# State-space layers on Trainium2: from tiles of 128 channels with one state per row to tiles of 32 channels by four states

## The chip, the cores and the metric

The kernel runs on one core of one Trainium2 chip. A core has five engines with instruction queues of their own: TensorE (PE, matrix products), VectorE (DVE), ScalarE (ACT, functions), GpSimd (POOL) and SyncE (SP, which here only issues DMA transfers). Each works through its queue strictly in order and waits on semaphores for the others. SBUF is the on-chip memory with 128 partitions (rows), PSUM the accumulator memory of TensorE, DRAM the memory outside. The metric is the device time of one execution in microseconds (us), and a kernel's time is the median of its runs.

## The reference

Eight images of 384 channels and 32 x 32 pixels go through four layers, each of the form x = x + f(norm(x)). Layers 0 and 2 are state-space (Mamba) layers; layer 2 has a two-matrix MLP behind it. Layer 1 is a deformable convolution and layer 3 a shift by rounded offsets with a small blur. Only layers 0 and 2 are changed. Cut to what matters, one of them is, for a sequence of 1024 tokens:

```python
u  = silu(causal_conv3(in_proj(x)))            # 768 channels
dt, B, C = x_proj(u)                           # 24, 16 and 16 values a token
dt = softplus(dt @ dt_proj_w.T + bias)         # 768 channels
h  = exp(dt[d] * A[d, n]) * h + (dt[d] * u[d]) * B[n]    # token by token, 16 states n
y[d] = sum over n of h[d, n] * C[n]
out = out_proj((y + D * u) * silu(z))
```

The line for h is a recurrence over the tokens for each of 768 x 16 pairs of channel d and state n. Everything is float32.

## The kernel before

The layers run one after the other. A state-space layer is worked in **half-samples**: 8 images by two halves of 512 tokens make 16 steps. In a step the 768 channels are 6 groups of 128, one channel a partition, and the 16 states are taken two at a time. So a step has 6 x 8 = 48 **units** (s, j, m): half-sample s, channel group j, state pair m. I call the eight units of one j a **block**; a layer has 96 blocks and 768 units. A tile of a unit is 128 partitions by 2 states by 512 tokens (128x1024).

One unit is this chain:

- `decays` (L434, ACT): two activations exp(dt * A), one for each state, into PSUM (tile `da`, two buffers).
- `inputs` (L440, POOL): dt*u (tile `du`) times the rows B of this pair (tile `bc`), into `db` (three buffers).
- `scan` (L445, DVE): the recurrence, one tensor_tensor_scan over 1024 elements.
- `with_c` (L461): the result times C, on DVE, or on POOL for the units m that the table `GP_C` names (0 and 4 in layer 0, 0 in layer 2).
- `add_pair` (L469, POOL, layer 2 only): for the units of `GP_ADD` (1, 2, 3, 5, 6) the two states are added into one half of the tile.
- `read_out` (L474, PE): the states are summed by products with the identity matrix that accumulate in the PSUM tile `y`; two products a unit, one where the pair was added. In layer 0 a product with diag(D) opens the sum.

In the second half of a sample, small operations (`first_token`, `carry`, `add_carry`) bring the last state of the first half in. All 16 rows of B and C of a step are broadcast to 128 partitions by eight DMAs of 1 MB (`load_bc`, L382), eight `bc` tiles in all.

The step sizes of a block are made by `dt_proj` (PE), `soft_exp` and `soft_ln` (ACT), `soft_rest` (DVE) and `soft_sum` (L408, three POOL operations; the second finishes `dt`, the third makes `du`). Both tiles stay in SBUF in the form in which the units use them.

The order on PE, DVE, ACT and POOL is the order of the program text. The unit loop runs the pipeline ahead by hand: in iteration i POOL does `inputs` of unit i + 3 and ACT `decays` of unit i + 2, while DVE does `scan` of unit i. All other work of the step (projections, convolution, norms, the MLP of the step before) is put into lists by `plan` (L592), indexed by the unit at which it is issued. For a block that begins at unit t, the step sizes for the block **two further on** are made at t + 6 to t + 10: `soft_sum` is in the POOL list at t + 10, behind that iteration's `inputs`. Their first users are `inputs` of unit t + 16, which POOL issues in iteration t + 13, and `decays` of the same unit, which ACT issues in iteration t + 14. SP issues the loads and stores.

Of the kernel before, what the change touches and what calls it, by code (L numbers as in the profile page):

```python
# [30 lines left out]
GP_C = {0: (((0, 4), (0, 4)), ((0, 4), (0, 4))), 2: (((0,), (0,)), ((0,), (0,)))}  # L31
GP_ADD = {0: (), 2: (1, 2, 3, 5, 6)}
# [3 lines left out]
KS = (3, 5, 7)  # L36
CPP = 8
# [39 lines left out]
Q_YN, Q_XN, Q_SRC, Q_ONE, Q_EPS, Q_K, Q_BIG = 0, 8, 9, 18, 19, 20, 23  # L77
# [14 lines left out]
class Net:  # L92
# [107 lines left out]
    def ssm_layer(self, li, src, dst, shift=None):  # L200
        tc, nc, ins = self.tc, self.nc, self.ins
        mlp = li == 2
        gp_c, gp_add = GP_C[li], GP_ADD[li]
        nhs = 4 if mlp else 6
        with ExitStack() as ctx:
# [36 lines left out]
            na = wp.tile([P, ND, NS], F32, name="na")  # L242

            def states():
                naf = na.rearrange("p d n -> p (d n)")
                nc.scalar.activation(naf, vec[:, V_A : V_A + ND * NS], AF.Exp)
                nc.vector.tensor_scalar(naf, naf, -1.0, -1e-20, ALU.mult, ALU.min)
# [5 lines left out]
            def w_in(o):  # L253
                if not mlp:
                    return win[:, :, o * P : (o + 1) * P]
                t = p2.tile([P, G, P], F32, name="winr", tag="winr", bufs=3)
                nc.sync.dma_start(out=t, in_=win_d[:, :, o * P : (o + 1) * P])
                return t

            def w_mid(src, k):  # L260
                t = p2.tile([P, k, W_MID // k], F32, name="wm", tag="wm", bufs=3)
                n = src.shape[2]
                nc.sync.dma_start(out=t[:, :, :n], in_=src)
                return t
# [61 lines left out]
            def inner(s, d):  # L326
# [4 lines left out]
                xn, w = s["xn"], w_in(d)  # L331
# [42 lines left out]
            def x_store(s):  # L374
                ps = s["ps_x"]
                dbc = s["dbc"] = p1.tile([RB, TS], F32, name="dbc")
                nc.scalar.copy(dbc, ps)
                bcd = s["bcd"] = self.dram.tile([2, NS, TS], F32, name="bcd", tag="bcd")
                nc.sync.dma_start(out=bcd.rearrange("t n l -> (t n) l"), in_=dbc[RK:RB, :])
                s["bc"] = {}  # L380

            def load_bc(s, m):  # L382
                bc = s["bc"][m] = p2.tile([P, 2, 2, TS], F32, name="bc", tag="bc", bufs=NS // 2)
                nc.sync.dma_start(out=bc, in_=s["bcd"][:, 2 * m : 2 * m + 2, :].partition_broadcast(P))
# [7 lines left out]
            def soft_exp(s, j):  # L392
                bias, ps = v(V_DB + j), s["ps_dt"]
                s["dt", j] = dt = p2.tile([P, TS], F32, name="dt", tag="dt")
# [13 lines left out]
            def soft_sum(s, j):  # L408
                dt = s["dt", j]
                s["du", j] = du = p2.tile([P, TS], F32, name="du", tag="du")  # L410
# [5 lines left out]

            def first_token(s, j):
                dt = s["dt", j]
                if s["h"] == 1:
                    s["a0"] = p1.tile([P, NS], F32, name="a0")  # L420
                    nc.scalar.activation(s["a0"], na[:, j, :], AF.Exp, scale=dt[:, 0:1])
                nc.scalar.activation(dt[:, 0:1], self.col(Q_BIG), AF.Identity)

            def carry(s, j):
                if s["h"] == 1:
                    nc.gpsimd.tensor_tensor(s["a0"], s["a0"], s["st"][:, j, :], ALU.mult)

            def add_carry(s, j, m):
                if s["h"] == 1:
                    d = s["db", m][:, :, 0:1]  # L430
                    nc.gpsimd.tensor_tensor(d, d, s["a0"][:, 2 * m : 2 * m + 2].unsqueeze(2), ALU.add)  # L431


            def decays(s, j, m):  # L434
                da = s["da", m] = dap.tile([P, 2, TS], F32, name="da", tag=f"da{m % 2}")
                for i in range(2):
                    n = 2 * m + i
                    nc.scalar.activation(da[:, i, :], s["dt", j], AF.Exp, scale=na[:, j, n : n + 1])  # L438

            def inputs(s, j, m):  # L440
                db = s["db", m] = p2.tile([P, 2, TS], F32, name="db", tag="db", bufs=3)
                du = s["du", j].unsqueeze(1).to_broadcast([P, 2, TS])
                nc.gpsimd.tensor_tensor(db, du, s["bc"][m][:, 0], ALU.mult)  # L443

            def scan(s, j, m):  # L445
# [3 lines left out]
                h = da  # L449
                if m in gp_c[s["h"]][j % 2]:  # L450
                    h = s["hs", m] = p2.tile([P, 2, TS], F32, name="hs", tag="hs", bufs=nhs)
# [4 lines left out]
            def keep_last(s, j, m):  # L456
                if s["h"] == 0:
                    h = s["h", m]
                    nc.scalar.copy(s["sib"]["st"][:, j, 2 * m : 2 * m + 2].unsqueeze(2), h[:, :, TS - 1 : TS])  # L459

            def with_c(s, j, m):  # L461
                c = s["bc"][m][:, 1]
                if m in gp_c[s["h"]][j % 2]:
                    nc.gpsimd.tensor_tensor(s["hs", m], s["hs", m], c, ALU.mult)  # L464
                else:
                    hs = s["hs", m] = p2.tile([P, 2, TS], F32, name="hs", tag="hs", bufs=nhs)
                    nc.vector.tensor_tensor(hs, s["da", m], c, ALU.mult)  # L467

            def add_pair(s, j, m):  # L469
                hs = s["hs", m]  # L470
                nc.gpsimd.tensor_tensor(hs[:, 0, :], hs[:, 0, :], hs[:, 1, :], ALU.add)  # L471


            def read_out(s, j, m):  # L474
                k = s["read"] = (s.get("read", -1) + 1) % NU
                first = k == 0
                if first:
                    s["y"] = yp.tile([P, TS], F32, name="y", tag="y")
                    if not mlp:
                        nc.tensor.matmul(s["y"], diag_d[:, j, :], s["u"][:, j, :], start=True, stop=False)  # L480
                        first = False
                n = 1 if m in gp_add else 2
                for i in range(n):
                    nc.tensor.matmul(  # L484
                        s["y"], self.ident, s["hs", m][:, i, :],
                        start=first and i == 0, stop=k == NU - 1 and i == n - 1,
                    )

            def z_proj(s, j):
                w = w_in(ND + j)  # L490
# [20 lines left out]
            def out_proj(s, o, k0, k1):  # L511
                if k0 == 0:
                    wo = w_mid(wout_d[:, :, o * P : (o + 1) * P], ND) if mlp else wout[:, :, o * P : (o + 1) * P]
                    s["out", o] = self.psum("ps_o"), wo
# [25 lines left out]
            def mlp_up(s, q, f):  # L540
                if f == 0:
                    s["w1"] = w_mid(w1_d[:, :, q * 4 * P : (q + 1) * 4 * P], G)
                s["up", f] = ps = self.psum("ps_h")
                for k in range(G):
                    nc.tensor.matmul(  # L545
                        ps, s["w1"][:, k, f * P : (f + 1) * P], s["t"][:, k, :], start=(k == 0), stop=(k == G - 1)
                    )

            def up_take(s, q, f):
                if f == 0:  # L550
                    if s is steps[-1] and q == 1:
                        t = p2.tile([P, 2, 2, TS], F32, name="hid1", tag="bc", bufs=NS // 2)
                        s["hid"] = t.rearrange("p a b l -> p (a b) l")
# [8 lines left out]
            def mlp_down(s, q, o):  # L562
                if o == 0:
                    s["w2"] = w_mid(w2_d[:, 4 * q : 4 * q + 4, :], 4)
                s["down", o] = ps = self.psum("ps_m")
                for f in range(4):
                    nc.tensor.matmul(  # L567
                        ps, s["w2"][:, f, o * P : (o + 1) * P], s["hid", q][:, f, :], start=(f == 0), stop=(f == 3)
                    )

            def down_take(s, q, o):
# [5 lines left out]
                if q == NF // 4 - 1:  # L577
                    store(s, o)

# [12 lines left out]
            def plan(prev, s, nxt):  # L592
# [6 lines left out]
                for j in range(ND):  # L599
                    t = NU * j  # L600
                    put(dve, t + 1, close, *((s, j - 1) if j else (prev, ND - 1)))
                    put(pe, (0, 9, 18, 27, 33, 41)[j], z_proj, s, j)
# [11 lines left out]
                    put(pool, t + 10, soft_sum, n, k)  # L614
                put(pe, 0, norm_load, nxt)
# [20 lines left out]
                for d, t in enumerate((15, 16, 17, 24, 25, 26)):  # L636
                    put(pe, t, inner, nxt, d)
# [5 lines left out]
                for m in range(NU):  # L643
                    put(pool, 41 + m, load_bc, nxt, m)
                put(act, 7 if mlp else 9, residual, prev)
                for o, (t, e) in enumerate(((1, 2), (3, 4), (5, 6)) if mlp else ((8, 9), (10, 11), (12, 13))):
                    put(pe, t, out_proj, prev, o, 0, ND // 2)
                    put(pe, e, out_proj, prev, o, ND // 2, ND)
                    put(act if mlp else dve, e + (1 if mlp else 2), out_take, prev, o)
                if mlp:  # L650
                    ups = ((7, 8, 11, 13), (22, 23, 28, 29), (37, 38, 39, 40))
                    downs = ((19, 20, 21), (34, 35, 36), (43, 44, 45))
                    for q, g in enumerate((17, 33, 42)):
                        for f, t in enumerate(ups[q]):
# [14 lines left out]
            with tc.manual_schedule(engines=ENGINES):  # L669
# [10 lines left out]
                for d in range(ND):  # L680
                    inner(s, d)
# [10 lines left out]
                for j in range(2):  # L692
                    for fn in (dt_proj, soft_exp, soft_rest, soft_ln, soft_sum):
                        fn(s, j)
                for m in range(NU):
                    load_bc(s, m)
# [8 lines left out]
                for i, (s, j, m) in enumerate(units):  # L705
# [10 lines left out]
                    mine = m in gp_c[s["h"]][j % 2]  # L716
                    for r in early.pop(i, ()):
                        read_out(*units[r])
# [20 lines left out]
                    if m in gp_add:  # L739
                        add_pair(s, j, m)  # L740
                    run(pool[t])
                    run(pe[t])
                    for r in late.pop(i, ()):
                        read_out(*units[r])
                    k = 3 if mine else 2 if m in gp_add else 1
                    (early if k > 1 or m == NU - 1 else late).setdefault(i + k, []).append(i)
                for r in sum((early.get(len(units) + k, []) for k in range(3)), []):
                    read_out(*units[r])
                close(s, ND - 1)
                residual(s)  # L750
                if mlp:
                    parts = self.shift_parts(wp, p2, dap, dst, *shift)
# [3 lines left out]
                    for i in range(6):  # L756
                        stat_load(i)
                    stats = list(range(last))
                for o in range(G):
                    out_proj(s, o, 0, ND)  # L760
                    out_take(s, o)
                if mlp:
                    kernels_a()

                    def some(n):
                        for _ in range(min(n, len(stats))):
# [3 lines left out]
                            if i + 6 < last:  # L770
                                stat_load(i + 6)
# [3 lines left out]
                    for q in range(NQ + 1):  # L775
                        if q < NQ:
                            for f in range(4):
# [1070 lines left out]
```

## Time and profile before

| what | value |
|---|---|
| median of 3 runs (lowest to highest) | 9387.92 us (9382.41 to 9391.77) |
| profiled execution: span from first to last instruction | 9392.0 us; no longer time is recorded for it |
| layer 0, units (62 to 2974 us) | 2912 us, 30.33 us a block |
| layer 2, units (5915 to 9112 us) | 3197 us, 33.30 us a block |
| busy share of the span: PE, DVE, ACT, POOL | 90%, 86%, 69%, 62% |
| DMA moved | 791.97 MB, 84 GB/s over the span |

The span is 4 us (0.04%) above the median, so a difference worked out on the profiled execution can be put on the median as it stands. The POOL share over the span is low because POOL has little to do in layer 1 (about 3000 to 5830 us); in the unit stages of the two state-space layers PE, DVE and POOL are all busy for around nine tenths of the time. A float32 product shows as two matmul instructions in the trace. PE's busy time is modelled, since its products overlap at their ends.

### The profile page before, as it was taken

Reading aid. Unit: us, or ns where it says so; the run is one execution under the profiler, and the core shown is the slowest. Engines: PE = TensorE matmul, PEld = TensorE weight load, DVE = VectorE, ACT = ScalarE, POOL = GpSimd, SP = SyncE. Lnnn points to the kernel's source line nnn. Section 1 sums busy time; section 2 is a strip of 40 time slices with the busy share of each in tenths; the row PEclk is TensorE's granted clock in tenths of the full one; section 3 lists DMA queues with packets and bytes.
Section 4 is the critical chain, followed back from the end, with each engine's and each line's share of the span. In section 5 each row is a group of like instructions: output and inputs, shape, how many; then the busy total and the mean of one; then the engine's idle time right before and its main releaser. Section 6 shows DMA issues by size and latency. Waiting matters only on the chain. (4 is left out here: it accounts for less than half of the span.)

```text
span 9392.0 us, 87221 instructions
## 1 busy us (share of the span) xinstructions
PE 8473.1 (90%) x27891; PEld 4507.2 (48%) x27916; DVE 8088.9 (86%) x8857; ACT 6489.3 (69%) x10147; POOL 5825.4 (62%) x3825
## 2 busy tenths in 40 slices
PE   7898888888887999999999997699999999999987
PEld 3333333333333677677777776244343443434333
DVE  7999999999996678778778777899999999999973
ACT  6666666666663778778778777667777777777750
POOL 7989999999896000000000000899999999999974
PEclk9999999999998999999999998799999999999998
DMA  2111211121121233333333333233232333322436
GB/s 98 63 57 47 85 57 50 58 81 53 50 82 45 74 82 87 90 81 88 90 83 87 90 80 92 88 103 99 92 95 88 119 116 97 94 92 91 126 98 128
DMA packets 566063, 791.97 MB, mean 84 GB/s; under 512 B 244242, under 2 KB 397234, under 8 KB 542040
## 3 DMA queue, kind: packets, MB, share of 16 engines
q1 hardware_dynamic: 503492, 775.85, 28.2%
q10 hardware_dynamic: 62100, 10.44, 0.6%
q8 instruction: 223, 3.65, 0.2%
q14 instruction: 248, 2.03, 0.1%
HBM read 716.49 MB, written 69.66 MB: 84 GB/s over the span
## 5 line engine op out<-in xcount | busy, mean ns | idle before, releaser
L443 POOL TENSOR_TENSOR db<-du,bc 128x1024 f32<-128x1024 f32 x1536 | 3607.7, 2356 | 290.0 <-DVE hs L453 164.1
L453 DVE TENSOR_TENSOR_SCAN da<-da,db 128x1024 f32<-128x1024 f32 x1248 | 2857.4, 2290 | 125.1 <-ACT da L438 64.1
L484 PE MATMUL y<-hs,ident 128*128 128x512 f32 x5184 | 2598.4, 637 | 377.5 <-DVE hs L467 216.9
L438 ACT ACTIVATE da<-dt,na 128x512 f32<-128x512 f32 x3072 | 2120.8, 691 | 812.2 <-DVE hs L467 665.2
L411 POOL TENSOR_TENSOR dt<-dt,sp_e 128x512 f32<-128x512 f32 x192 | 244.3, 1272 | 2929.8 <-DVE sp_e L403 2929.8
L484 PEld LDWEIGHTS y<-hs,ident 128*128 128x128 f32 x5184 | 1013.1, 202 | 1853.0 <-issue 1094.2
L1516 PE MATMUL wacc<-fsm,fxk 128*128 128x221 f32 (+34 forms) x10624 | 1658.9, 315 | 96.5 <-DVE fsm L1486 93.8
L1516 PEld LDWEIGHTS wacc<-fsm,fxk 128*128 128x128 f32 x10624 | 1571.3, 195 | 234.9 <-DVE fsm L1486 157.6
L467 DVE TENSOR_TENSOR hs<-da,bc 128x1024 f32<-128x1024 f32 x1248 | 1528.5, 1225 | 91.6 <-DVE da L453 1.4
L1486 DVE TENSOR_TENSOR fsm<-fhy,fhx 128x170 f32<-128x170 f32 (+42 forms) x3216 | 1173.1, 436 | 342.9 <-PE wacc L1516 315.6
L1446 ACT ACTIVATE fhy<-fpyx,cell 128x416 f32<-128x416 f32 (+9 forms) x1280 | 646.8, 578 | 383.5 <-DVE fsm L1486 383.5
L1469 DVE TENSOR_TENSOR fxk<-fxt,fwk 128x1024 f32<-128x1024 f32 (+1 forms) x688 | 789.4, 1186 | 10.3 <-ACT fxt L1248 10.3
L453 DVE TENSOR_TENSOR_SCAN hs<-da,db 128x1024 f32<-128x1024 f32 x288 | 656.9, 2281 | 52.0 <-POOL db L431 35.8
L464 POOL TENSOR_TENSOR hs<-hs,bc 128x1024 f32<-128x1024 f32 x288 | 678.7, 2356 | 32.7 <-ACT st L459 32.3
L471 POOL TENSOR_TENSOR hs<-hs 128x512 f32<-128x512 f32 x480 | 610.0, 1271 | 4.6 <-DVE hs L467 4.1
L545 PE MATMUL ps_h<-t,wm 128*128 128x512 f32 x1152 | 538.5, 605 | 16.8 <-DVE x L574 16.6
L567 PE MATMUL ps_m<-hid,wm 128*128 128x512 f32 x1152 | 525.3, 600 | 20.1 <-ACT hid L560 17.2
L1451 ACT ACTIVATE fhy<-fhy,cols 128x1344 f32<-128x1344 f32 (+10 forms) x368 | 531.4, 1444 | 12.0
L459 ACT COPY st<-da 128x2 f32<-128x2 f32 x624 | 98.2, 157 | 512.0 <-DVE hs L467 509.8
L1157 PE MATMUL ps_off<-fxn,fow 128*98 128x465 f32 (+10 forms) x896 | 386.6, 579 | 0.0
L1433 ACT ACTIVATE fhx<-fpyx,cell 128x544 f32<-128x544 f32 (+8 forms) x640 | 380.7, 668 | 0.0
L567 PEld LDWEIGHTS ps_m<-hid,wm 128*128 128x128 f32 x1152 | 217.3, 192 | 314.8 <-issue 252.5
(203 smaller groups left out, 9866.3 us busy)
## 6 DMA issues: line engine op xcount, KB each, us to landing
bc<-bcd SPq DMA_DIRECT2D x256, 1024.0 KB
fpyx<-fposd SPq DMA_DIRECT2D x640, 256.0 KB
wm<-in_w SPq DMA_DIRECT2D x96, 768.0 KB
x<-x SPq DMA_DIRECT2D x71, 768.0 KB
winr<-in_win SPq DMA_DIRECT2D x192, 192.0 KB
x<-in_x SPq DMA_DIRECT2D x40, 768.0 KB
fpyx<-fposd SPq DMA_DIRECT2D x24, 1024.0 KB
wm<-in_wout SPq DMA_DIRECT2D x48, 384.0 KB
```

Source lines behind the costliest of these rows:

```text
L438: nc.scalar.activation(da[:, i, :], s["dt", j], AF.Exp, scale=na[:, j, n : n + 1])
L443: nc.gpsimd.tensor_tensor(db, du, s["bc"][m][:, 0], ALU.mult)
L453: nc.vector.tensor_tensor_scan(h1, da1, db1, 0.0, ALU.mult, ALU.add)
L464: nc.gpsimd.tensor_tensor(s["hs", m], s["hs", m], c, ALU.mult)
L467: nc.vector.tensor_tensor(hs, s["da", m], c, ALU.mult)
L471: nc.gpsimd.tensor_tensor(hs[:, 0, :], hs[:, 0, :], hs[:, 1, :], ALU.add)
L484: nc.tensor.matmul(s["y"], self.ident, s["hs", m][:, i, :], start=first and i == 0, stop=k == NU - 1 and i == n - 1,)
L567: nc.tensor.matmul(ps, s["w2"][:, f, o * P : (o + 1) * P], s["hid", q][:, f, :], start=(f == 0), stop=(f == 3))
L1446: nc.scalar.activation(hy[:, at : at + (yb - ya) * W], pyx[:, 0, ya * W : yb * W], AF.Abs, bias=bias)
L1469: nc.vector.tensor_tensor(t[:, :n], x, wk[:, j : j + 1, :].to_broadcast([P, n, P]), ALU.mult)
L1486: nc.vector.tensor_tensor(self.sub(sm, at, [(r * w, n), (w, r), (1, w)]), self.sub(hy, hy_at[by] + xa, [(r * W, n), (W, r), (1, w)]), self ...
L1516: nc.tensor.matmul(a[:, ya - 4 * o : yb - 4 * o, xa:xb], k, self.sub(sm, sm_at[by], [(w, yb - ya), (1, w)]), start=False, stop=False,)
```

## The change

The same 768 units a layer are cut differently. A tile now holds **four states by 32 channels** on the partitions and two further states along the free dimension; unit m = (p, k) covers channels 32k to 32k + 31 of the block's 128 and the eight states of half p. The elementwise operations of a unit keep their shapes (128x1024, two 128x512 activations).

- `dt` and `du` of a block are needed on every quarter of the partitions for four sub-blocks of 32 channels. `spread` stores both to DRAM (two stores of 256 KB) and loads each four times, to partitions 0 to 31, 32 to 63, 64 to 95 and 96 to 127 (eight loads of 256 KB in rows of 2 KB), into `dtb` and `dub`, two buffers each. It stands in the POOL list at t + 11, and SP issues its ten DMAs.
- `load_bc` brings only the four state rows that a quarter needs: two tiles a step, each by four loads of 256 KB. `bc` has three buffers instead of eight.
- `read_out` runs once for each half p, when its four units are done: eight products of a constant 128x32 selection matrix with the tiles. Product k writes partitions 32k to 32k + 31 of `y`, so four products use four column groups of PE. A block has 16 of them in both layers. `add_pair` is gone.
- `GP_C` is now 0 and 4 in layer 0, as before; in layer 2 it is 0, 2, 4 for even blocks and 0, 4 for odd ones.
- The loads of weight tiles (`fetch_in`, `fetch`) are issued two units ahead of the products that use them. `first_token` in a second half does four exponentials instead of one. `hs` has seven buffers. Tiles of layer 3 that lay in the `bc` buffers now rotate through the `bc`, `dtb` and `dub` buffers; five loads run ahead there instead of six.

The core of the diff:

```diff
-GP_C = {0: (((0, 4), (0, 4)), ((0, 4), (0, 4))), 2: (((0,), (0,)), ((0,), (0,)))}
-GP_ADD = {0: (), 2: (1, 2, 3, 5, 6)}
+NI = 4
+IP = P // NI
+NSUB = P // IP
+NQP = NS // NI // 2
+GP_C = {0: ((0, 4), (0, 4)), 2: ((0, 2, 4), (0, 4))}
...
-            def load_bc(s, m):
-                bc = s["bc"][m] = p2.tile([P, 2, 2, TS], F32, name="bc", tag="bc", bufs=NS // 2)
-                nc.sync.dma_start(out=bc, in_=s["bcd"][:, 2 * m : 2 * m + 2, :].partition_broadcast(P))
+            def load_bc(s, p):
+                bc = s["bc"][p] = p2.tile([P, 2, 2, TS], F32, name="bc", tag="bc", bufs=3)
+                for i in range(NI):
+                    nc.sync.dma_start(
+                        out=bc[i * IP : (i + 1) * IP].rearrange("p t q l -> p (t q) l"),
+                        in_=s["bcd"][i, p].partition_broadcast(IP),
+                    )
...
+            def spread(s, j):
+                raw = self.dram.tile([2, P, TS], F32, name="dtd", tag="dtd")
+                for k, name in enumerate(("dt", "du")):
+                    nc.sync.dma_start(out=raw[k], in_=s[name, j])
+                for k, name in enumerate(("dtb", "dub")):
+                    t = s[name, j] = p2.tile([P, NSUB, TS], F32, name=name, tag=name)
+                    v = raw[k].rearrange("(s d) l -> d s l", d=IP)
+                    for i in range(NI):
+                        nc.sync.dma_start(out=t[i * IP : (i + 1) * IP], in_=v)
...
             def inputs(s, j, m):
+                p, k = divmod(m, NSUB)
                 db = s["db", m] = p2.tile([P, 2, TS], F32, name="db", tag="db", bufs=3)
-                du = s["du", j].unsqueeze(1).to_broadcast([P, 2, TS])
-                nc.gpsimd.tensor_tensor(db, du, s["bc"][m][:, 0], ALU.mult)
+                du = s["dub", j][:, k, :].unsqueeze(1).to_broadcast([P, 2, TS])
+                nc.gpsimd.tensor_tensor(db, du, s["bc"][p][:, 0], ALU.mult)
...
-            def add_pair(s, j, m):
-                hs = s["hs", m]
-                nc.gpsimd.tensor_tensor(hs[:, 0, :], hs[:, 0, :], hs[:, 1, :], ALU.add)
...
+            def read_out(s, j, p):
+                if p == 0:
                     s["y"] = yp.tile([P, TS], F32, name="y", tag="y")
                     if not mlp:
                         nc.tensor.matmul(s["y"], diag_d[:, j, :], s["u"][:, j, :], start=True, stop=False)
+                for i in range(2):
+                    for k in range(NSUB):
+                        nc.tensor.matmul(
+                            s["y"][k * IP : (k + 1) * IP, :], sel, s["hs", p * NSUB + k][:, i, :],
+                            start=mlp and p == 0 and i == 0, stop=p == NQP - 1 and i == 1,
+                        )
...
                     put(pool, t + 10, soft_sum, n, k)
+                    put(pool, t + 11, spread, n, k)
...
-                for m in range(NU):
-                    put(pool, 41 + m, load_bc, nxt, m)
+                for p, t in enumerate((36, 45)):
+                    put(pool, t, load_bc, nxt, p)
...
                 for j in range(2):
-                    for fn in (dt_proj, soft_exp, soft_rest, soft_ln, soft_sum):
+                    for fn in (dt_proj, soft_exp, soft_rest, soft_ln, soft_sum, spread):
                         fn(s, j)
-                for m in range(NU):
-                    load_bc(s, m)
+                    load_bc(s, j)
```

## The prediction

> **What bounds the kernel now.** I read the stretches first, then the groups of POOL, then POOL's queue of one block in order of time, last the DMA. The change touches two stretches; their busy times (us of the stretch, then of each engine):
>
> ```profile
> core 0: us, PE busy (x) PEld busy (x) DVE busy (x) ACT busy (x) POOL busy (x), PEclk, DMA share, GB/s
> 62.00:2974.00 2912.00, 2554.76 (x5526) 1057.73 (x5527) 2704.96 (x1842) 1910.30 (x3225) 2660.53 (x1674) 0.93 0.17 59
> 5915.00:9112.00 3197.00, 2981.25 (x6721) 1247.38 (x6722) 3006.45 (x2213) 2327.64 (x3678) 3028.68 (x2059) 0.97 0.32 98
> ```
>
> Divided by 96 blocks, layer 0 takes 30.33 us a block, with DVE busy 28.2, POOL 27.7, PE 26.6; layer 2 takes 33.30, with DVE 31.3, POOL 31.5, PE 31.1. So no engine binds alone: three queues are nearly full and coupled by three `db` and two `da` buffers. A wait of some microseconds in each block, on POOL above all, therefore reaches the end. In layer 0 only 2.6 us a block of POOL's time are free.
>
> Now POOL's queue around the making of step sizes, in layer 0 (start, us, operation):
>
> ```profile
> 1661.65 1.26 POOL L411 TENSOR_TENSOR dt<-dt,sp_e 128x512 f32<-128x512 f32 x1
> 1662.99 1.27 POOL L412 TENSOR_TENSOR dt<-dt,sp_w 128x512 f32<-128x512 f32 x1
> 1664.34 1.27 POOL L413 TENSOR_TENSOR du<-dt,u 128x512 f32<-128x512 f32 x1
> 1665.57 4.65 POOL L443 TENSOR_TENSOR db<-du,bc 128x1024 f32<-128x1024 f32 x2
> 1670.19 2.34 POOL L464 TENSOR_TENSOR hs<-hs,bc 128x1024 f32<-128x1024 f32 x1
> 1672.50 4.66 POOL L443 TENSOR_TENSOR db<-du,bc 128x1024 f32<-128x1024 f32 x2
> ```
>
> By the program's order the rows behind L413 are `inputs` of units t + 14 and t + 15, `with_c` of t + 12, and at 1672.50 `inputs` of t + 16, the first user of the `du` that was finished at 1665.6. There is no idle time between. So POOL comes for the new `du` **6.9 us** after making it. Before, it lies there in SBUF. After, it has to have been to DRAM and back by then.
>
> **What the change removes and saves.** DVE and POOL in layer 0: nothing (same shapes, same `GP_C`). Layer 2, POOL: five `add_pair` a block at 1.271 us (610.0 us over 480) go, -6.4 us; 1.5 more `with_c` at 2.36 come, +3.5. DVE there loses 1.5 at 1.225, -1.8 us. PE: a float32 product is two instructions of 0.443 us, 0.886 together (the pace of `ps_in`: 180 instructions in 79.7 us between 7000 and 8000). Layer 0 has 16 + 1 a block, layer 2 has 11. The 16 of 128x32 take a quarter of the time if four run side by side. This trace has such products in layer 1, also float32, four column groups of 32:
>
> ```profile
> 3037.33 5.95 PE L1195 MATMUL ps_off<-fxn,fow 128*32 128x256 f32 x72 [2.04 <-issue]
> ```
>
> 72 instructions in 5.95 us are 83 ns each, at a granted clock of 0.67 in that stretch. One after the other, at 256 columns, they would take about 222 ns each at full clock; so they do run side by side. PE then has about 4 x 0.9 = 3.5 us a block instead of 14.2 or 9.7. PE stops being near the bound; that alone frees only the DVE waits on `y` and `ps_o` (18 and 13 us in a millisecond of layer 0).
>
> The page "TensorE: Matmul & The Clock Gate" of the Trainium skill (Part 3) is less generous: it gives 2.38x for three column tiles of 32, not 3x. By that factor the read-out would be 14.2 / 2.38 = 6 us a block as an estimate, still off the path, and the sum below would not move.
>
> **What it adds, and where it lies.** For each block SP issues two stores and eight loads. The time A from the finished `du` to the landed `dub` is built so, with 0 at the end of L412 (`dt` final):
>
> ```profile
> 49.07 0.33 SPq L379 DMA_DIRECT2D bcd<-dbc  x1
> 50.72 8.87 SPq L384 DMA_DIRECT2D bc<-bcd  x8
> ```
>
> This is the same path, a store to DRAM whose reader waits for it on SP: 64 KB need 1.65 us until the load is issued. For 256 KB I add 192 KB at the rate of a store in 2 KB rows:
>
> ```profile
> 1404.00:1405.00 1.00, 1.00 (x4) 0.38 (x3) 1.00 (x2) 0.51 (x1) 0.00 (x0) 1.00 0.00 0
> 1405.00:1406.00 1.00, 1.00 (x4) 0.49 (x3) 1.00 (x1) 0.97 (x3) 0.00 (x0) 1.00 0.95 365
> 1406.00:1407.00 1.00, 1.00 (x3) 0.38 (x2) 0.32 (x1) 0.97 (x3) 0.60 (x1) 1.00 1.01 377
> ```
>
> That store was issued at 1404.15; its first bytes move 0.85 us later, then 371 GB/s (last column). So: `dt` stored at 1.65 + 0.5 = 2.2; first bytes of `dtb` at 2.2 + 0.85 = 3.05. `du` is finished 1.35 after `dt` (start to start of L412 and L413), stored by 1.35 + 2.2 = 3.55, and its four loads queue behind those of `dtb` on the same engines. Both are 2.097 MB. The rate: the loads of layer 3 (`sxr`) also go to 32 partitions each, 256 KB at a time, all four quarters in turn:
>
> ```profile
> 9202.00:9204.00 2.00, 2.00 (x11) 2.00 (x11) 0.00 (x0) 0.00 (x0) 0.00 (x0) 0.50 1.14 196
> 9206.00:9208.00 2.00, 1.79 (x2) 0.84 (x3) 1.50 (x5) 0.00 (x0) 0.00 (x0) 0.50 1.13 202
> 9214.00:9216.00 2.00, 2.00 (x6) 0.95 (x5) 1.25 (x1) 0.00 (x0) 2.00 (x2) 1.00 1.14 204
> ```
>
> 200 GB/s, with the DMA engines full (share above 1). Their rows are 1 KB, ours 2 KB. The bounds are 371 GB/s (2 KB rows over 128 partitions) and 194 (the slowest stretch of these loads, at 9210). I take 200, since the 32 partitions are what the two have in common. Then 2.097 MB take 10.5 us, until 13.55, and the landing comes 0.6 later (what the 1.65 of the small store leaves beside 0.85 and 64 KB at 371): 14.15 after `dt`, so **A = 12.8 us** after `du`. Bounds: 7.95 (371 GB/s) and 13.1 (194). `dtb` itself has landed at about 8.9; ACT asks for it 10 us after `dt` (first use of `dt` at 1674.24 by `first_token`), so `decays` are in time. The buffers add no wait: with two of each, the ones that are filled held the block that `inputs` left at iteration t + 4 and `decays` at t + 5.
>
> The Trainium skill bears on the rate, in "SBUF — State Buffer", "Door 1: The DMA port swizzle": partitions 0 to 31 reach 8 of 16 ports, measured there at 189 GB/s against 328, and two DMAs to different halves gained 6%. It speaks against the quarter loads; by its 189 A would be 13.4 and the time some 115 us more than my sum.
>
> **The cycle.** `dub` arrives; POOL does six `inputs` (t + 16 to t + 21), one `with_c`, then the next `soft_sum`; that gives the next `du`, and A begins again. So a block cannot be shorter than A plus that POOL work. In layer 0 it is 1693.17 - 1672.50 = 20.7 us in the trace, less 0.5 idle, plus 1.0 for the carries (L426 and L431 take 83 us and 26 us of gaps over the layer's 96 blocks, nearly all in this part): 21.2. Layer 2: 6 x 2.31 + 1.5 x 2.31 + 3.95 + 1.0 = 22.3.
>
> - Layer 0: 12.8 + 21.2 = 34.0 against 30.33: +3.67 x 96 = **+352 us**.
> - Layer 2: 12.8 + 22.3 = 35.1 against 33.30: +1.8 x 96 = **+173 us**. What it saves on POOL is spent waiting.
> - Prologue of each layer: the first `inputs` stand at 61.96 and would wait for the first `dub` (56.5 + 14) and perhaps a `bc` load behind it: 8 to 14, +22 for both.
> - Nothing for: `bc` (2 MB a step instead of 8, behind the spreads in SP's queue and first used four units or more after their issue; with that cover gone, up to 5 us each, two a step), the three extra exponentials in odd halves (0.3 us each; ACT has 10 us a block free), the earlier weight loads (no engine waits for weights now), five loads ahead instead of six in layer 3 (bounds 0 and +10; the DMA is full there either way).
>
> Sum: 9392 + 352 + 173 + 22 = 9939; on the median, 4 lower, **9935 us**. What is queued behind the waiting POOL operation is all of POOL; DVE waits for `db`, ACT for DVE, and PE for both.
>
> **The rivals.**
>
> 1. Faster: the quarters overlap. If loads to different quarters use the engines together and run near 371 GB/s, A is 7.95 and POOL waits only 1 us. Then DVE binds: layer 0 at 28.2 busy falls to about 29.6 (PE's waits gone), -67; layer 2 at 29.5 busy and the present 94% goes to 31.4, -178; with the prologue 9392 - 223 = 9169. It decides where A is under 9.1 in layer 0 and 11.0 in layer 2; both together break even near A = 10. For it: 2 KB rows, half as many packets as `sxr`. Against: three stretches at 200 with full engines. 20%.
> 2. SP blocks. Weight loads, `residual` and `bc` stand in the same queue, and layer 2 moves 98 GB/s already. If a spread starts 2 to 3 us late in each block, A is 15 and both layers lose 2.2 x 96 more: 10355. For it: SP waited for engines 715 us on `bc` alone (L384 on POOL). Against: most of those waits end when a buffer comes free, with SP idle before. 10%.
> 3. The column groups run one after the other: PE in layer 2 gets 5 x 0.886 = 4.4 us a block more, 35.5 busy, and about 36 a block: +259 there instead of +173, 10020. Against it is the row of L1195. 5%.
>
> **Numbers.** Forecast case 65%, its own range 9690 to 10090 (A from 11.5 to 13.6, a little past the bound of 13.1 for other traffic). Rivals 20, 10 and 5%. The measurement tells 0.2% (19 us) from no change. Faster: 20% (rival 1, less a little). Same: 3%, since it needs A near 10. Slower: 77%. For 8 in 10 the range runs from 9150, the case of overlap, to 10150.
>
> **What would show it.** Right: POOL idle before L443 by some 5 to 6 us a block, released by DMA `dub`; the DMA near 200 GB/s and full while it waits; DVE at about 84% in both layers; no `add_pair`; 1.2 us or less for four read-out products. Wrong: if POOL waits for `dub` less than 2 us a block, the rate or the latency was over-priced, and then the time is under the old one. If ACT waits for `dtb`, the order of the loads is another than I read.

## The result and the profile after

The changed kernel takes **10096 us** (median of four runs, 10078 to 10105) against 9390 (9382 to 9394): ratio **1.075**, 95% interval 1.074 to 1.077. The forecast was 9935, with a range of 9150 to 10150.

The stretches of the profile after: layer 0 from its first scan to its last, layer 2 likewise, and what lies behind the last scan.

```profile
core 0: us, PE busy (x) PEld busy (x) DVE busy (x) ACT busy (x) POOL busy (x), PEclk, DMA share, GB/s
75.00:3353.00 3278.00, 2071.45 (x5522) 604.72 (x5522) 2703.38 (x1841) 1944.98 (x3369) 2652.73 (x1674) 0.77 0.42 99
6311.00:9781.00 3470.00, 2686.96 (x7672) 986.77 (x7672) 2829.28 (x2067) 2343.03 (x3822) 2766.78 (x1722) 0.89 0.54 133
9781.00:10090.30 309.30, 234.20 (x520) 103.59 (x520) 110.87 (x190) 26.23 (x34) 100.72 (x48) 0.87 0.61 130
```

DVE and POOL do in layer 0 what they did (2703 and 2653 us of work) in a stretch that is 369 us longer, so that time is waiting. PE lost nearly 500 us of work there and nothing got faster for it. POOL's queue shows the wait, at the place where the profile before had no gap between L413 and the third `inputs`; SP's rows of the same stretch stand below it:

```profile
1664.74 1.27 POOL L429 TENSOR_TENSOR du<-dt,u 128x512 f32<-128x512 f32 x1
1665.97 2.34 POOL L482 TENSOR_TENSOR db<-dub,bc 128x1024 f32<-128x1024 f32 x1
...
1679.76 4.65 POOL L482 TENSOR_TENSOR db<-dub,bc 128x1024 f32<-128x1024 f32 x2 [6.31 <-DMA dub<-dtd]
```

```profile
1664.69 0.34 SPq L436 DMA_DIRECT2D dtd<-dt  x1
1666.04 0.34 SPq L436 DMA_DIRECT2D dtd<-du  x1
1666.43 0.42 SPq L397 DMA_DIRECT2D bc<-bcd  x1
1666.94 1.80 SPq L441 DMA_DIRECT2D dtb<-dtd  x4
1668.84 1.80 SPq L441 DMA_DIRECT2D dub<-dtd  x4
```

`du` is finished at 1666.0 and `inputs` of the new block starts at 1679.8, after 6.31 us idle: this A is 13.8 us. In between the DMA is full at the rate that was forecast for quarter loads:

```profile
1672.00:1674.00 2.00, 0.49 (x3) 0.20 (x6) 2.00 (x2) 0.00 (x0) 1.45 (x1) 0.50 1.06 202
1674.00:1676.00 2.00, 1.43 (x6) 0.00 (x0) 1.90 (x2) 1.17 (x6) 0.00 (x0) 0.50 1.08 210
1676.00:1678.00 2.00, 1.36 (x8) 0.38 (x9) 0.59 (x1) 1.97 (x4) 0.00 (x0) 0.50 1.08 214
```

Over the whole span the group of `inputs` says it in one line, 1235 us idle before it, 1115 of them ended by DMA `dub`:

```profile
L482 POOL TENSOR_TENSOR db<-dub,bc 128x1024 f32<-128x1024 f32 x1536 | 3591.0, 2354 | 1235.4 <-DMA dub<-dtd 1114.7
```

The 698 us between the two spans by place: layer 0's units +369, layer 2's +279, the starts of both layers +25 (the first scan comes 10.9 us later, and 13.9 us more lie between the layers), the end +26.

### The profile page after: what moved, and what is told of

Read it like the earlier page. It is cut to its first block, busy times and chain, and to the rows that moved or that the text cites. A ratio compares the mean times of both kernels' runs of the same rounds, so it can differ in the third digit from the quotient of the medians.

```text
span 10090.3 us, 91894 instructions
## 1 busy us (share of the span) xinstructions
PE 7704.8 (76%) x28851; PEld 3793.6 (38%) x28876; DVE 7911.8 (78%) x8713; ACT 6536.8 (65%) x10435; POOL 5559.9 (55%) x3489
## 5 line engine op out<-in xcount | busy, mean ns | idle before, releaser
L482 POOL TENSOR_TENSOR db<-dub,bc 128x1024 f32<-128x1024 f32 x1536 | 3591.0, 2354 | 1235.4 <-DMA dub<-dtd 1114.7
L474 ACT ACTIVATE da<-dtb,vec 128x512 f32<-128x512 f32 x3072 | 2117.7, 691 | 1086.5 <-DVE hs L494 510.4
L494 DVE TENSOR_TENSOR_SCAN da<-da,db 128x1024 f32<-128x1024 f32 x1104 | 2526.5, 2288 | 119.3 <-ACT da L474 45.8
L517 PE MATMUL y<-hs,cols 128*32 128x512 f32 x6144 | 1317.8, 733 | 778.0 <-POOL hs L505 465.8
L494 DVE TENSOR_TENSOR_SCAN hs<-da,db 128x1024 f32<-128x1024 f32 x432 | 986.1, 2283 | 989.8 <-POOL db L467 579.1
L507 DVE TENSOR_TENSOR hs<-da,bc 128x1024 f32<-128x1024 f32 x1104 | 1351.6, 1224 | 61.0 <-DVE da L494 0.9
L505 POOL TENSOR_TENSOR hs<-hs,bc 128x1024 f32<-128x1024 f32 x432 | 1017.8, 2356 | 15.3 <-ACT st L500 15.3
L517 PEld LDWEIGHTS y<-hs,cols 128*32 128x32 f32 x6144 | 222.7, 119 | 1776.7 <-DVE hs L507 640.9
L549 PE MATMUL ps_o<-u,wm 128*128 128x512 f32 x576 | 328.4, 724 | 126.2 <-DVE u L537 77.4
L526 PE MATMUL ps_z<-xn,winr 128*128 128x512 f32 x576 | 310.8, 682 | 112.6 <-ACT da L474 68.7
```

Of the source, the lines that this page charges most:

```text
L474: nc.scalar.activation(da[:, i, :], s["dtb", j][:, k, :], AF.Exp, scale=na[:, j, n + i : n + i + 1])
L482: nc.gpsimd.tensor_tensor(db, du, s["bc"][p][:, 0], ALU.mult)
L494: nc.vector.tensor_tensor_scan(h1, da1, db1, 0.0, ALU.mult, ALU.add)
L507: nc.vector.tensor_tensor(hs_tile(s, m), s["da", m], c, ALU.mult)
L517: nc.tensor.matmul(s["y"][k * IP : (k + 1) * IP, :], sel, s["hs", p * NSUB + k][:, i, :], start=mlp and p == 0 and i == 0, stop=p == NQP - ...
```

## The experiments

In the table, a layer's time from its first scan to its last is divided by 96. A is the mean over the blocks that the trace shows whole, from the end of `du` (L429) to the first `inputs` of its block; it is given where POOL waits for `dub` in at least half of the blocks; elsewhere it is mostly the time that POOL takes to get there, and is left out.

| kernel | median us | ratio to before (95%) | layer 0, us a block | A | layer 2, us a block | A |
|---|---|---|---|---|---|---|
| before | 9388 to 9392 | 1 | 30.30 | | 33.24 | |
| the change | 10096 | 1.075 (1.074 to 1.077) | 34.14 | 13.3 | 36.15 | 13.9 |
| e1 three units earlier | 9484 | 1.010 (1.008 to 1.011) | 29.91 | | 34.14 | |
| e2 dub first | 9921 | 1.056 (1.054 to 1.058) | 32.74 | 9.7 | 35.76 | 10.3 |
| e3 every fourth partition | 9579 | 1.019 (1.018 to 1.021) | 31.35 | 10.4 | 33.73 | 11.0 |
| e4 by sub-blocks | 11276 | 1.201 (1.199 to 1.203) | 39.63 | 17.4 | 42.68 | 17.5 |
| e5 two units earlier | 9379 | 0.999 (0.998 to 1.000) | 30.59 | 13.9 | 32.25 | |
| e6 e3 and e4 in one | 9267 | 0.987 (0.985 to 0.989) | 29.66 | 8.3 | 32.12 | 8.3 |
| e7 e5 and e6 in one | 9273 | 0.987 (0.986 to 0.989) | 29.44 | | 32.42 | |
| e8 e1, wide read-out | 9643 | 1.027 (1.025 to 1.028) | 31.52 | | 34.01 | |
| e9 e6 without DRAM | 9278 | 0.988 (0.986 to 0.989) | 29.58 | 8.1 | 32.30 | 7.8 |
| e10 e6, layer 0 earlier | 9256 | 0.986 (0.984 to 0.988) | 29.45 | | 32.14 | 8.4 |
| e11 one unit later | 10649 | 1.134 (1.132 to 1.136) | 37.06 | 13.2 | 39.02 | 14.0 |
| e12 e10, six ahead | 9246 | 0.985 (0.983 to 0.986) | 29.45 | | 32.21 | 8.4 |

**Theory:** a block is A plus POOL's work from the landing of `dub` to the next `du`. **Rivals:** SP's queue and the DMA volume set the pace wherever the spread is put; or the engines work slower (PE's granted clock fell from 0.93 to 0.77 in layer 0).

### e1 and e11: the step sizes earlier and later

```diff
-                    put(pool, t + 10, soft_sum, n, k)
-                    put(pool, t + 11, spread, n, k)
+                    put(pool, t + 7, soft_sum, n, k)
+                    put(pool, t + 8, spread, n, k)
```

`dt_proj`, `soft_exp`, `soft_rest` and `soft_ln` move with them. In e11 all six move by one unit the other way.

> Step sizes are made and spread three units earlier (t + 3 to t + 8 in place of t + 6 to t + 11); nothing else is changed. Theory (POOL waits for the way of du through DRAM, A = 13.2 us in layer 0 and 13.9 in layer 2, before each block): three units give about 11 us more of POOL work between the finished du and its first use, 6 to 7.5 + 11 = 17 to 18.5 us, so the wait goes and the units are set by DVE again: 29.6 to 30 us a block in layer 0, 31.4 to 32 in layer 2, in all 10096 - 96 x 4.4 - 96 x 4.6 = 9230 us, 9150 to 9300. Rival 1 (SP's queue and the DMA volume hold every block up): the loads come late wherever they are put, and the time stays above 9600. Rival 2 (not a wait, but the engines work slower, PE at a lower clock above all): no change, 10096 within 30.

> The change as it is, but step sizes are made and spread one unit later (t + 7 to t + 12). Theory (a block is A plus the POOL work from the landing of dub to the next du): A stays at 13.3 and 13.9 us, and that work holds one more inputs, 2.33 us, so both layers lose 2.33 us a block: 10096 + 2.33 x 192 = 10540 us, 10450 to 10600. Rival (the volume of the spreads and SP's queue set the pace): within 50 of 10096. If the wait were a fixed price a block that no order of POOL's work changes, also 10096.

In e1 POOL hardly waits for `dub`, and layer 0 is at 29.91 us a block, as the theory had it; both rivals fall for that layer (the clock is still 0.77). Layer 2 missed its number: 34.14 where 31.4 to 32 was expected. What is late next there, from PE's waits in layer 2 of e1:

```profile
PE ps_o L549 <- DMA wm<-in_wout: 148.8, 7, 25.0
```

The spread of a step's last block now stands in SP's queue ahead of the first weights of `out_proj` for the step that begins, at seven of the step changes.

e11 lies 109 us above its 10540 and outside the range up to 10600, on the theory's side: A stays (13.2 and 14.0) and the blocks grow by 2.9 us, where one `inputs` is 2.33. Most of the other 0.6 us is a wait that the sum left out: between the landing of `dub` and the next `du`, POOL waits for DVE (L494) 0.65 us a block in layer 0 and 0.40 in layer 2, where it was 0.04 and 0.02 in the change.

### e5: two units earlier

The same lines with t + 8 and t + 9, so that the spread stands behind those weight loads.

> Step sizes are made and spread two units earlier (t + 4 to t + 9), one unit less than in e1; nothing else is changed. In e1 the spread of a step's last block stood in the iteration in which the next step begins, ahead of the loads of the output weights, and PE waited 21 to 25 us for wm at each second step of layer 2, 149 us in all, with POOL and DVE behind it. Here that spread stands one iteration behind those loads. Theory: the two units give 2 x 3.7 us and 2 x 4.1 us on top of 7.2 us, so the way through DRAM (13.3 and 13.9 us) is still covered, barely in layer 2; layer 0 stays at 29.9 to 30.1 us a block and layer 2 loses the wait for wm: 34.1 to 32.3, in all 9340 us, 9290 to 9430. Rival (the DMA volume of layer 2, 150 GB/s with half of the loads at half rate, is what costs): layer 2 stays above 33.9 and the whole above 9460. Second rival: two units are too few, dub is waited for again in both layers, above 9500.

9379 is within the expected range, but only half for the expected reason: the wait for `wm` at L549 is no longer among PE's nine longest and layer 2 falls to 32.25, while layer 0 rises to 30.59. There two units are too few: POOL waits 138 us for `dub`.

### e2: dub ahead of dtb

```diff
-                for k, name in enumerate(("dtb", "dub")):
+                for k, name in ((1, "dub"), (0, "dtb")):
```

> The four loads of dub are issued ahead of those of dtb; nothing else is changed. Theory: dub no longer queues behind 1 MB that takes 5.2 us at 200 GB/s, so A falls to 8.0 us in layer 0 and 8.7 in layer 2 and POOL's cycle to 29.2 and 31.0, under DVE's floor. Then dtb lands last and ACT, which asks for it about one unit later than POOL for dub, waits 1 to 2 us a block: 30.7 us a block in layer 0, 32.5 in layer 2, in all 9385 us, 9250 to 9550. Rival 1 (SP's queue): SP has the same ten issues to make, so the gain is under a third of that, above 9850. Rival 2 (engines slower): no change, 10096 within 30.

A fell by 3.6 us, not 5.2, and the time by 176 us, not 710. The sum had made ACT the waiter, but at 1 to 2 us a block. Three rows of e2's waits (total, times, longest):

```profile
ACT a L448 <- DMA dtb<-dtd: 493.2, 86, 10.2
ACT dtb L452 <- DMA dtb<-dtd: 439.4, 86, 10.0
...
DVE hs L494 <- ACT da L474: 574.9, 158, 8.6
```

Over the two layers, ACT waits for `dtb` in 172 blocks, 5.4 us each. Both tiles are on the path; their order mostly chooses which engine waits. The time lies where the expectation put its first rival (above 9850), but these rows name the loads of `dtb` and not SP's issues as what is waited for. Why A fell by 3.6 us only was not traced.

### e3: every fourth partition

```diff
-                        nc.sync.dma_start(out=t[i * IP : (i + 1) * IP], in_=v)
+                        nc.sync.dma_start(out=t[i::NI], in_=v)
```

`bc` is loaded in the same way; the selection matrix and the table of A follow the new order.

> The four states of a channel lie on neighbouring partitions (partition 4 d + i in place of 32 i + d), so each quarter load of dtb, dub and bc writes every fourth partition from 0 to 127; sizes, rows, number and order of the DMAs stay, and the selection matrix and the table of A follow. Theory that the half rate comes from a load reaching only 32 neighbouring partitions: the 2.1 MB run near the 371 GB/s of the x store, 5.7 us in place of 10.5, A is 8.4 and 9.1 us, 29.6 to 30 us a block in layer 0 and 31.4 to 32 in layer 2, in all 9200 us, 9150 to 9350. Rival, that the rate comes from the rows of 2 KB, from four loads of one source or from SP's issue: no change, 10096 within 50. A rate between the two shows as 52 us of time for each 0.27 us of A.

Same bytes, rows and number of transfers, at another rate (stretches of two microseconds in one block of e3, last column GB/s):

```profile
1658.00:1660.00 2.00, 0.00 (x0) 0.00 (x0) 2.00 (x2) 1.98 (x3) 1.62 (x2) 1.00 0.85 282
1660.00:1662.00 2.00, 0.00 (x0) 0.00 (x0) 1.74 (x2) 1.96 (x4) 1.55 (x2) 0.75 0.95 330
1662.00:1664.00 2.00, 0.40 (x2) 0.19 (x4) 1.46 (x1) 1.91 (x4) 1.54 (x1) 0.50 1.03 371
```

So the half rate did come from 32 neighbouring partitions, but the new rate is some 330 GB/s (the mean of these rows) and not 371, and A falls to 10.4 and not 8.4. The cycle then still binds: 10.4 + 21 = 31.4 against 31.35 measured. The time misses its number by 380 us because A stayed above the 9 us at which the wait would vanish; the law that joins the two held.

### e4 and e6: one sub-block in each load

```diff
+                    for q in range(NSUB):
+                        nc.sync.dma_start(
+                            out=t[:, q, :], in_=raw[k, q * IP : (q + 1) * IP].partition_broadcast(NI)
+                        )
```

That is e4, on the change's layout. e6 has the layout of e3, and the source `v.unsqueeze(1).to_broadcast([IP, NI, TS])`: 32 channels outside, four copies inside.

> Each of the four loads of dtb and of dub brings one sub-block of 32 channels to all 128 partitions (the source repeated four times), in place of four sub-blocks to one quarter of the partitions; bytes, rows and the number of DMAs stay. The first inputs of a block then needs one load of dub, not four, and the first decays one load of dtb. Theory: A ends with the first dub load: 13.2 less three quarters of dub's 5.2 us is 9.3 us at the old rate and 6.5 at 371 GB/s; the cycle with 21.2 us of POOL work is 30.5 or 27.7, so layer 0 falls to 29.6 to 30.6 us a block, layer 2 to 31.5 to 32.6, in all 9200 to 9400 us. Rival 1 (SP's queue): the first dub load is issued when it was, and the gain is under a third, above 9800. Rival 2 (engines slower): no change.

> As e4, each load of dtb and dub brings one sub-block of 32 channels to all partitions, but on the layout of e3 (partition 4 d + i), so that the outer count of the transfer is 32 channels and not 4 copies; step sizes are made when the change makes them. Theory (e4 was slow because a transfer with an outer count of 4 ran on 4 of 16 DMA engines: share 0.26, 98 GB/s): the loads run at the 310 GB/s of e3; the first inputs needs the first load of dub, the fifth of eight, so A is e3's 10.4 less 3 x 0.85 = 7.9 us in layer 0 and 8.4 in layer 2; the cycle with 21 us of POOL work is 29 us and no longer binds. Layer 0 at 29.9 to 30.2 us a block, layer 2 at 32 to 33, in all 9310 us, 9230 to 9420. Rival (a load by sub-blocks is slow for another reason, such as the source read four times): A above 12, time above 9900.

e4 is 1180 us slower than the change, where its theory and its rivals had a faster or an unchanged kernel. Its DMA while POOL waits, and SP's issue of the same block:

```profile
1744.00:1746.00 2.00, 1.54 (x6) 0.00 (x0) 1.90 (x2) 0.21 (x1) 0.00 (x0) 0.50 0.26 98
```

```profile
1737.59 2.22 SPq L440 DMA_DIRECT2D dtb<-dtd  x4
1739.91 10.11 SPq L440 DMA_DIRECT2D dub<-dtd  x4
```

A share of 0.26 is about four of 16 engines: with the four copies as the outer count, each transfer went to four engines, at 98 GB/s, and the issue of the next four took SP 10 us. "DMA: Bandwidth & Descriptors" of the Trainium skill states this in "Rules for kernel authors": an outermost dimension of c < 16, its example a leading repeat of c copies, keeps the whole transfer on at most c engines. The row agrees. e6 turns the two counts, which goes with the layout of e3, and keeps the rest of e4's idea. Its loads run on all engines:

```profile
1664.00:1666.00 2.00, 0.00 (x0) 0.00 (x0) 1.91 (x1) 1.47 (x3) 2.00 (x2) 0.50 0.81 264
1666.00:1668.00 2.00, 0.66 (x3) 0.37 (x6) 1.97 (x3) 0.31 (x3) 1.29 (x1) 0.50 1.00 356
```

A is 8.3 us, `dub` is waited for 123 us in all, in 118 blocks, and **e6 is 1.3% faster than the kernel before** (ratio 0.985 to 0.989).

### e7, e10, e9, e12: what is left beyond e6

e7 is e6 with step sizes two units earlier; e10 does that in layer 0 alone (`sooner = 0 if mlp else 2`); e9 reads the loads of e6 from the SBUF tiles `dt` and `du`, without the stores; e12 is e10 with `AHEAD = 6`.

> e5 and e6 together: spread two units earlier, and by sub-blocks over all partitions. Theory: the way through DRAM is hidden with 7 us to spare and the transfers take 6 us of the DMA engines a block in place of 10.5, so weights pass too: layer 0 at DVE's floor of 29.6 to 30, layer 2 at 31.5 to 32.5, in all 9250 us, 9180 to 9330. If e5 and e6 have each removed the whole wait, this one is no faster than the better of the two by more than 40 us.

> e6 with the two units of e7 in layer 0 alone. From the stages of the two profiles: layer 0 of e7 (2826.6 us) and layer 2 of e6 (3083.6), so 21 us less than e6: 9246 us, 9235 to 9262. It tests whether the gain of e7 in layer 0 and its loss in layer 2 (waits of DVE for sp_w and of POOL for a) belong to the layers and not to the run.

> e6 without the way through DRAM: the four loads of dtb and the four of dub read the tiles dt and du in SBUF, 32 source partitions each, repeated four times; the two stores are gone. Theory: the 2.2 us between a store and its loads go, A falls from 8.3 to 6 us and no block waits for dub any more (48 us in layer 0 and 72 in layer 2 in e6); DVE is busy 94% there, so under half of that comes back: 9267 - 20 to - 60 = 9225, 9200 to 9255. Rival (a source of 32 neighbouring partitions is read at half rate, as such a target was written): the loads take 10 us in place of 6, A is 9 or more, and the time is 9267 to 9350.

> e10 with six loads ahead in layer 3, as the kernel before had it, in place of five. It prices the term of the prediction that was put at 0 to +10 us (five loads ahead): behind the last scan of layer 2 the kernel before takes 283 us, the change and all its variants 308 to 312. Theory (five loads ahead and the smaller set of buffers start the first or the following loads later): the end falls back to 283 to 290 and the whole to 9256 - 20 to - 27 = 9232 us. Rival (the end is longer for another reason, such as the buffers' order or the loads behind the last step's weights): no change, 9256 within 8.

e7 is not faster than e6: layer 0 gains 21 us, layer 2 loses 28, with new waits such as POOL for `a` from ACT (63 us in layer 2) and DVE for `sp_w` (44 us). e10 repeats both stages to 1 and 2 us of what was put together; its total is not separated from e6's by the intervals. In e7 no block waits for `dub` any more. So what those waits cost in e6 is about 20 us of layer 0, and DVE is busy 95% of that layer.

In e9 the saved way through DRAM is eaten by a slower load: A is 8.1 and 7.8 in place of 8.3, and POOL still waits for `dub` in 115 blocks, where none was expected to. Two stretches of its loads, which read 32 neighbouring partitions each:

```profile
1664.00:1666.00 2.00, 0.00 (x0) 0.00 (x0) 1.98 (x1) 1.08 (x2) 2.00 (x1) 0.50 0.93 214
1666.00:1668.00 2.00, 1.82 (x5) 0.37 (x6) 1.99 (x2) 0.73 (x5) 0.73 (x2) 0.50 0.86 201
```

The two microseconds before them ran at 258 GB/s; over the whole transfer, in the 39 blocks of layer 0 that have no other load nearby, the 2.1 MB take some 10.5 us. That is about 200 GB/s, near the quarter loads' 202 to 214, and in e6 they take some 7 us. The rival was right on the rate and on the time (9278), not on A (9 or more); the two effects cancel. That the 32 neighbouring partitions are the reason, and not the reading of SBUF in place of DRAM, is not shown: no run reads SBUF in another pattern.

In e12 the end is 296 us, against 283 before and 309 after: half of the 26 us came back. POOL's waits there for the stores of layer 3, in the kernel before, the change and e12:

```profile
POOL sxa L1701 <- DMA out<-sxr: 26.7, 3, 9.9
```

```profile
POOL sxa L1753 <- DMA out<-sxr: 72.7, 9, 10.3
```

```profile
POOL sxa L1754 <- DMA out<-sxr: 45.2, 5, 9.6
```

The other half stays open. As a whole e12 (9246) is not told from e10 by the intervals.

### e8: the read-out without column groups

```diff
-                            s["y"][k * IP : (k + 1) * IP, :], sel, s["hs", p * NSUB + k][:, i, :],
+                                s["y"], selw[:, o : o + P], s["hs", p * NSUB + k][:, i, :],
```

`selw` is `sel` with zeros on both sides, `o = P - (k + 1) * IP`; layer 0 only.

> e1 with the read-out of layer 0 by 128x128 products, as before the change: the 32 columns of the selection matrix stand in a matrix that is zero elsewhere, so each product writes all 128 rows of y and no two run side by side; layer 2 keeps column groups. It prices what the column groups give once the wait for dub is gone. PE gets 16 x 0.886 - 3.7 = 10.5 us a block more, about 28 of 30. Theory (DVE and POOL bind layer 0, PE was not the bound): layer 0 goes from 29.9 to 30.2 to 30.5, about the 30.3 of the kernel before, in all +30 to +60 us on e1's 9484. Rival (the column groups are what makes layer 0 faster than before): +150 us or more. No effect at all would say that PE is free in either form.

Layer 0 goes from 29.91 to 31.52 us a block, +155 us: the rival of that expectation. Sixteen instructions (eight products), in the change and then in e8, both at a granted clock of 1.00:

```profile
1631.96 1.92 PE L517 MATMUL y<-hs,cols 128*32 128x512 f32 x16
```

```profile
1647.91 7.03 PE L527 MATMUL y<-hs,selw 128*128 128x512 f32 x16
```

Seven microseconds in one piece hold up PE's other products, and DVE waits for them (84 us for `y`, 57 for `ps_o`; neither is among its longest waits in e1). It is slower than the 30.30 of the kernel before, which spread as many products over eight units; how much is the width and how much the burst was not separated.

## Why the prediction was right, point by point

- **The number:** 10096 is 161 us above 9935 and 6 us outside the forecast case's own range (9690 to 10090); the wider range covers it. By stretches of the profile, layer 2 gives 106 us of the miss, the end 26, layer 0 17 and the starts 3.
- **What bounds:** right. No engine binds alone, and POOL's wait reaches the end: 5.5 us a block in layer 0 and 6.1 in layer 2 released by `dub`, where 5 to 6 were named, and DVE is busy 82% of both layers, where 84 were. e1 takes the wait away and layer 0 falls below the old time; e11 lengthens the work behind a constant A and the time follows.
- **The cycle, A plus POOL's work:** layer 0 13.3 + 20.9 for the 12.8 + 21.2 of the sum; its term of +352 measured +369. That it came so near is in part luck: A was half a microsecond too low and POOL's work 0.3 us too high.
- **Layer 2's term was mis-sized:** +279 for +173. POOL's work is as it was put (36.15 - 13.9 = 22.25 for 22.3); the whole error is A, 13.9 for 12.8, and 1.1 x 96 = 106. I sorted the waiting blocks by whether another load was issued between `du`'s store and the loads of `dub`. Without one A is 12.9 in layer 0 (60 of 89 blocks) and 12.8 in layer 2 (34 of 88): the forecast number. With one it is 14.2 and 14.7, and layer 2 has such a load in 54 of 88, `winr` or `wm` in 41. One of them, SP's rows and then POOL's, with an A of 15.2 us:

```profile
8064.54 0.34 SPq L436 DMA_DIRECT2D dtd<-du  x1
8064.98 0.39 SPq L275 DMA_DIRECT2D wm<-in_wout  x1
8065.47 2.01 SPq L441 DMA_DIRECT2D dtb<-dtd  x4
8067.57 2.71 SPq L441 DMA_DIRECT2D dub<-dtd  x4
```

```profile
8063.26 1.26 POOL L429 TENSOR_TENSOR du<-dt,u 128x512 f32<-128x512 f32 x1
...
8079.72 9.31 POOL L482 TENSOR_TENSOR db<-dub,bc 128x1024 f32<-128x1024 f32 x4 [8.30 <-DMA dub<-dtd]
```

  The step that failed is "Nothing for ... the earlier weight loads (no engine waits for weights now)": `dub` waits behind their bytes, whatever else waits for them. They make 0.9 us of the 1.1; the other 0.2 are quarter loads of `bc`, for which the same line put nothing either. In layer 0 the load in front is always one of these `bc` loads, of 256 KB: at 200 GB/s that is 1.3 us as an estimate, and 1.3 us is what A grows by there. It is the second rival's mechanism at about a quarter of its price. All this is read from the trace of the change; no run takes these loads out of the way.
- **A sign of being wrong:** "If ACT waits for `dtb`, the order of the loads is another than I read." ACT does wait for it in the change, 115 times and 320 us in all. In the block of layer 0 shown above:

```profile
1674.76 0.86 ACT L448 ACTIVATE a<-vec,dtb 128x4 f32<-128x4 f32 x4 [3.73 <-DMA dtb<-dtd]
```

  The order was read rightly: in these blocks `inputs` of the new `dub` starts 5.1 us later still, so ACT's wait is not the one that ends last. What was off is the times: `dtb` was put at 8.9 us after `dt`, with ACT asking at 10; where ACT waits, it asks at 7.1 to 7.5 and has the tile at 9.9 to 10.4.
- **The rate:** 200 GB/s as taken, 202 to 214 measured. e3 shows the reason that was chosen (32 neighbouring partitions) to be the right one.
- **The starts:** +25 for +22. **The end:** +26, where five loads ahead was put at nothing with a bound of 10; e12 shows half of it to be that, and the bound was too narrow.
- **The first rival** named a faster end at A under 9, 9169 us. The condition was right: e6 has A = 8.3 and is faster than before. The price was 100 us too optimistic, mostly in layer 2 (32.1 us a block, not 31.4) and at the end.
- **The third rival** fell: four products take 0.96 us when they come in one piece at a clock of 1.00. The read-out as a whole is busier than the 3.5 us a block that were put: L517 is busy 1317.8 us over the 192 blocks, 6.9 us each. In pieces and at a lower clock its products take longer, such as ten instructions in 3.62 us at 1676.64, with the clock at 0.50. The sum does not use this term. "PE stops being near the bound; that alone frees only the DVE waits" may have been too small a view: e8 costs 155 us in layer 0, more than the 75 us that DVE waits for `y` and `ps_o` there in the kernel before, but part of that can be the burst. The Trainium skill's 2.38x ("TensorE: Matmul & The Clock Gate", Part 3) is for three column tiles; four gave 7.03 / 1.92 = 3.7 here.

## What to carry to other kernels

When a tile that stayed on chip is sent through DMA, write down the time from its finish to its first use in the queue that uses it; what the round trip exceeds that by is paid in every block, and an engine made idle elsewhere gives nothing back. Then either make the tile earlier, and look at which loads it now stands in front of, or cut the round trip, by the partitions that a load reaches and by what its first user needs. In a queue with other loads, put a price on the bytes ahead, not only on who waits for them.

## What the runs showed of the hardware beyond that

- 256 KB loads to 32 neighbouring partitions ran at 202 to 214 GB/s with full DMA engines; the same loads to every fourth partition at 282 to 371 (the change, e3). Loads from 32 neighbouring partitions of SBUF to all 128 gave about 200 over a block (e9).
- The order of the counts in a repeated source decides how many DMA engines work: share 0.26 and 98 GB/s with 4 outside (e4), 0.81 to 1.00 and 258 to 356 GB/s with 32 outside (e6).
- Four column groups of float32 products run 3.7 times as fast as four full-width ones (1.92 against 7.03 us for eight products in one piece, both at a granted clock of 1.00).
- The granted clock was lower where PE had gaps: 0.93 in layer 0 before, 0.77 with PE busy 63% of the stretch, 0.92 again in e8 with PE busy 85%. e1 has 0.77 as well, and its blocks in layer 0 are shorter than those of the kernel before (29.91 against 30.30 us).
